# Second stage of blocks 2 and 3: where VectorE's sums for the next block, ScalarE's modulation pairs and one PSUM copy stand in their engines' orders

## Chip, core and metric

The kernel runs on one core of one Trainium2 chip. The metric is the device time of one execution in microseconds (us). Before the change it is 259.0 us (median of three runs, 258.9 to 259.67). All arithmetic is in fp32.

## What is computed

`x` holds 64 batches of 64 tokens with 512 features, 4096 token rows in all. Cut to what matters:

```python
q  = relu(cond @ W3 + b3)                          # 64 x 512
v  = (64 * x + x.sum(tokens)) * q[:, None, :]      # "modulation"
y  = relu(v @ W2 + b2)                             # first product, 512 x 512
g  = softmax(y @ W_router + b_router)              # 6 experts
w  = g kept for the two best experts, else 0
out = x + y @ W_base + b_base + (y @ A_s) @ B_s \
        + sum over experts e of w[e] * (y @ A_r[e]) @ B_r[e]
```

There are two large products, with W2 and with W_base. The rest is narrow: rank 16 for each of seven groups, six router columns.

## The kernel before, in words

Features lie on the 128 partitions, so the 512 features are four chunks; token rows lie along the free dimension. The rows are worked in four blocks (the loop over `k`, 0 to 3) of 1024 rows, two halves of 512. A block has a **first stage** (`first_inner`: modulated x times W2, then relu into `y`) and a **second stage** (the narrow product `ph`, the gate, and y times W_base plus the routed part).

Both large products use the seven-multiplication (Strassen-Winograd) form on 2x2 blocks, P1 to P7. In blocks 2 and 3 most of these P are themselves made by seven products of quarter blocks. In the code, `order` lists the outer products, `t` counts them, and `q(n, t)` is inner product n of the t-th one: two fp32 matmuls of 128x128 by 128x256 in the trace. Each outer product owns two PSUM banks, `ha`/`hb` in the second stage (`ia`/`ib` in the first). Its parts leave PSUM through small steps of `inner_tools`: `seed_y` (L987) and `seed_z` (L990) copy a half bank on ScalarE so that later products add to it; `take_w5`, `take_u`, `take_11`, `take_21` (all through `take`, L995) copy a quarter to SBUF on ScalarE; `take_12` and `take_22` (through `add`, L972) add a quarter on VectorE. TensorE may only overwrite or add to a quarter when the step that reads it is done.

The price of that form are sums of operands. For y they are made by GpSimd (`inner_sums`, L344 to L347) and VectorE (`row_sums`, L280 to L283). The sums for the **next** block's first stage, and the modulation of the next block's x, have no place of their own: they are put between the second stage's instructions. Two lists hold them.

* `behind` holds ScalarE's modulation, mostly in pairs (two activations, L229, each 128x64). `fill(n)` (L293) emits the next n entries.
* `held` holds VectorE's part: sums over tokens (`vsum`, L219 and L221), row sums `s` of feature chunk 0 (`early`, four instructions of 128x512, L280 to L283), the four inner sums `first` (128x256, L344 to L347), eight modulation steps of 128x64 (L227), three row sums of chunk 1, and four inner sums of 128x768 (L344 to L347). `sums_ahead(n)` (L298) emits the next n. One of the 28 entries allots two tiles and emits nothing.

The order is written by hand: each engine executes its instructions in the order in which the program emits them, and waits on semaphores for the others. There is no planner.

`second_between` (L712) is the second stage of blocks 2 and 3; its `main_part` (L785) is what the change edits. With `order = (1, 2, 4, 5, 3)`, t = 0 is P1, t = 1 is P2, t = 2 is P4, t = 3 is P5 and t = 4 is P3. P6 and P7 are plain products (`oy`, `oz`, L181) that are seeded with P1 by ScalarE (`seed`, L752). `with_x` adds x on VectorE and sends a row out on SyncE's queue. `to_rows` (L742) adds a finished P to the output rows in HBM by an accumulating DMA from GpSimd's queue; the second one adds to the rows of the first, so it waits until that has landed. `turn` transposes the weighted narrow product (`pt`, L647) and copies it to `hwT` (L649); `difference` (L654) is GpSimd's. Block 4 has no next block; it uses `second_inner`, which shares `inner_tools` only.

Of the kernel before, what the change touches and what calls it, by code (L numbers as in the profile page):

```python
# [38 lines left out]
def adaln_ffn(ctx: ExitStack, tc: tile.TileContext, xa, x0, x1, head, w3, w2, wb, a, bcat, bb, br, outT):  # L39
# [139 lines left out]
    def product(ps, i, j, w, s, start=True):  # L179
        for c in range(KH):  # L180
            nc.tensor.matmul(  # L181
                ps, w[i][:, c, ts(j, P)], s[i][:, c, :], start=start and c == 0, stop=c == KH - 1,
                skip_group_check=True,
            )
# [87 lines left out]
    def row_sums(a, name, cols=slice(0, TB)):  # L272

        all_s = mid.tile([P, 4, KH, TB], F32, tag=name, name=name)
        s = [all_s[:, i, :, cols] for i in range(4)]
        a11, a12, a21, a22 = a[:, :KH, 0, cols], a[:, KH:, 0, cols], a[:, :KH, 1, cols], a[:, KH:, 1, cols]

        def steps(c=slice(0, KH), fourth=nc.vector):
            return [
                lambda: nc.vector.tensor_tensor(s[0][:, c], a21[:, c], a22[:, c], ALU.add),  # L280
                lambda: nc.vector.tensor_tensor(s[1][:, c], s[0][:, c], a11[:, c], ALU.subtract),
                lambda: nc.vector.tensor_tensor(s[2][:, c], a11[:, c], a21[:, c], ALU.subtract),
                lambda: fourth.tensor_tensor(s[3][:, c], a12[:, c], s[1][:, c], ALU.subtract),  # L283
            ]

        return {1: a11, 2: a12, 3: s[3], 4: a22, 5: s[0], 6: s[1], 7: s[2], "sums": all_s}, steps
# [6 lines left out]
    def fill(n):  # L293
        for _ in range(min(n, len(behind))):
            for step in behind.pop(0):
                step()

    def sums_ahead(n):  # L298
        for _ in range(min(n, len(held))):
            held.pop(0)()  # L300
# [342 lines left out]
    def turn(k):  # L643
        pt = ps_h.tile([P, 2 * NS, P], F32, tag="ph", name=f"pt_{k}")
        hwT = small.tile([P, 2, TB], F32, tag="hwT", name=f"hwT_{k}")
        for s in range(2 * NS):
            nc.tensor.transpose(pt[:GB, s, :], hw[:, s, :], ident)  # L647
        for h in range(2):
            nc.scalar.copy(hwT[:GB, h], pt[:GB, ts(h, NS)].rearrange("p s t -> p (s t)"))  # L649
        return hwT  # L650

    def difference(k, hwT):
        hwd = small.tile([P, TB], F32, tag="hwd", name=f"hwd_{k}")
        nc.gpsimd.tensor_tensor(hwd[:GB], hwT[:GB, 0], hwT[:GB, 1], ALU.subtract)  # L654
        return hwd
# [56 lines left out]
    def second_between(k, y, res):  # L712


        order = (1, 2, 4, 5, 3)
        lo, hi = slice(0, R2), slice(R2, TB)
        of_y = {1: y[:, :KH, 0], 2: y[:, KH:, 0], 4: y[:, KH:, 1]}
        x12, x21, x22 = res[1, 0], res[0, 1], res[1, 1]
        plain = mid.tile([P, 4, 4, R2], F32, tag="inner_s", name=f"inner_y_{k}")
        sy, sy_steps = row_sums(y, "sy")  # L720
        sy_steps = sy_steps()

        of_sy = lambda n: sy["sums"][:, n].rearrange("p k t -> p (k t)").rearrange("p (n t) -> p n t", n=4)
        places = {o: plain[:, n] for n, o in enumerate((1, 2, 4))} | {5: of_sy(1), 3: of_sy(2)}
        s_side, sums_of = row_places(lambda o: of_y.get(o, sy[o]), {o: (t, (0, 1, 2, 3)) for o, t in places.items()})
        parts = {1: wide["parts"][:, 0], 2: wide["parts"][:, 1], 4: y[:, :KH, 1], 5: y[:, :KH, 0], 3: y[:, KH:, 0]}
        tools = inner_tools(k, "h", order, wide["t"], s_side, dict.fromkeys(order), parts)
        q, open_banks, bank, add = tools.q, tools.open_banks, tools.bank, tools.add
        hws = {}
        routed_of = {2: ("first", 0), 4: ("second", 0), 5: ("second", KH), 3: ("less", KH)}  # L730
        routed = with_routed(order, tools, hws, routed_of)

        def run(steps):
            for step in steps:
                step()

        def inner_sums(o):
            a = of_y.get(o, sy[o])
            run(sums_of(o, lambda c, r: a[:, c, ts(r, R2)], nc.gpsimd))

        def to_rows(o, f, h):
            nc.gpsimd.dma_start(  # L742
                outT[k, f : f + KH, h].rearrange("f p t -> p f t"), parts[o], accum_op=ALU.add
            )

        def with_x(x, name, j, f, h):
            add(x[:, j], bank[name, j], x[:, j])
            nc.sync.dma_start(outT[k, f + j, h], x[:, j])

        def seed(j, name, source):  # L750
            bank[name, j] = ps_p.tile([P, TB], F32, tag="pp", name=f"o{name}_{k}_{j}")
            nc.scalar.copy(bank[name, j], source)  # L752

        def start(t):
            open_banks(t)
            q(1, t)
            q(5, t)
            tools.seed_y(t)
            tools.take_w5(t)

        def sixth(t):
            q(6, t)
            tools.seed_z(t)
            tools.take_u(t)

        def seventh(t):
            q(7, t)
            routed(t, 22)
            tools.take_22(t)

        def second_and_third(t):
            q(3, t)
            q(2, t)

        def ends(t):
            routed(t, 1)
            tools.take_1(t)
            q(4, t)
            routed(t, 4)
            tools.take_21(t)  # L780

        for o in (1, 2):
            inner_sums(o)

        def main_part(ph):  # L785
            open_banks(1)
            q(1, 1)
            q(5, 1)
            tools.seed_y(1)

            def first():
                q(7, 0)
                q(3, 0)
                q(6, 1)
                tools.seed_z(1)
                q(2, 0)
                tools.take_11(0)
                tools.take_w5(1)
                tools.take_22(0)

            gate(k, ph, (first, lambda: tools.take_12(0)))
            q(4, 0)
            tools.take_21(0)
            second_and_third(1)
            weigh(k, ph)
            for j in range(KH):
                seed(j, "y", parts[1][:, j])
                product(bank["y", j], 6, j, tb, sy, start=False)
            fill(2)
            tools.take_u(1)  # L810
            sums_ahead(2)
            for j in range(KH):
                seed(j, "z", bank["y", j])
                with_x(x12, "y", j, KH, 0)

            for o in (5, 4):
                inner_sums(o)
            fill(2)
            product(bank["z", 0], 7, 0, tb, sy, start=False)
            with_x(x22, "z", 0, KH, 1)  # L820
            with_x(x21, "z", 0, 0, 1)
            hwT = turn(k)
            hws["first"], hws["second"] = (hwT[:GB, h] for h in range(2))
            product(bank["z", 1], 7, 1, tb, sy, start=False)
            with_x(x22, "z", 1, KH, 1)
            seventh(1)
            with_x(x21, "z", 1, 0, 1)
            hws["less"] = difference(k, hwT)[:GB]
            inner_sums(3)
            start(2)  # L830
            fill(2)
            ends(1)
            to_rows(1, 0, 0)
            to_rows(2, 0, 0)
            sums_ahead(4)
            sixth(2)
            fill(2)
            start(3)
            seventh(2)
            sums_ahead(5)  # L840
            second_and_third(2)
            sixth(3)
            fill(2)
            ends(2)
            to_rows(4, 0, 1)
            sums_ahead(8)
            start(4)
            seventh(3)
            sums_ahead(3)
            second_and_third(3)  # L850
            sixth(4)
            ends(3)
            to_rows(5, KH, 0)
            to_rows(5, KH, 1)
            sums_ahead(1)
            seventh(4)
            sums_ahead(3)
            second_and_third(4)
            ends(4)
            last_part.append(lambda: to_rows(3, KH, 0))  # L860

        return {
            "sums": lambda: run(sy_steps), 6: lambda: start(0), 7: lambda: sixth(0), "all": main_part
        }
# [515 lines left out]
```

## Time and profile before

| | |
|---|---|
| median of three runs | 259.0 us |
| the profiled execution, its own time | 258.9 us |
| its span from first to last instruction | 257.1 us |
| TensorE busy | 249.0 us (97%) |
| VectorE busy | 201.8 us (79%) |
| ScalarE busy | 156.5 us (61%) |
| GpSimd busy | 123.6 us (48%) |
| granted TensorE clock | 0.999 |
| block 2's stretch from its narrow product to the next first stage | 94.6 to 133.0 us |
| block 3's | 156.4 to 194.8 us |

PE is TensorE's matmul, PEld its weight load, DVE is VectorE, ACT ScalarE, POOL GpSimd, SP SyncE. A line of the timeline gives the start within the span, the duration, the engine, the source line, what is written from what, the shape, the number of instructions merged in the row, and in brackets the idle time just before and what ended it. Ends of matmuls are modelled, so two following rows of PE overlap by some 0.16 us. A row's duration on an engine also contains the time in which the instruction, once started, waits for something inside.

### The profile page before, as it was taken

What the parts mean: (1) busy time and instruction counts of PE and PEld (TensorE: products, weight loads), DVE (VectorE), ACT (ScalarE), POOL (GpSimd) and SP (SyncE); (2) the same over time, 40 slices, a digit from 0 to 9 for tenths busy, and PEclk for the clock granted to TensorE, in tenths of its full rate; (3) what the DMA queues carried; (4) which work ended last, traced back from release to release, by engine and by line L of the source; (5) the groups of instructions that cost most, each with busy time, mean ns of one, the idle gap of its engine ahead of it and who ended that gap; (6) DMA issues with size and microseconds to landing.
All of it is one profiled execution on the core that took longest, in us unless ns stands there. A gap on an engine that the chain in (4) does not pass through costs nothing.

```text
span 257.1 us, 3663 instructions
## 1 busy us (share of the span) xinstructions
PE 249.0 (97%) x1126; PEld 188.0 (73%) x1126; DVE 201.8 (79%) x405; ACT 156.5 (61%) x435; POOL 123.6 (48%) x150
## 2 busy tenths in 40 slices
PE   7999999999999999999998999999999999999994
PEld 3756896454467889657886888956788889975783
DVE  2899898699995887876897777996789576787472
ACT  2399496596049798767636889675855427442220
POOL 1000000029408686079269778219539995039850
PEclk9999999999999999999999999999999999999999
DMA  6998636003220044843598522305559553500054
GB/s 197 361 346 310 263 112 214 0 3 122 97 107 0 14 149 147 308 176 113 82 167 162 82 83 98 125 25 204 86 87 193 93 96 142 166 1 0 3 184 144
DMA packets 17339, 33.82 MB, mean 132 GB/s; under 512 B 1590, under 2 KB 3638, under 8 KB 17319
## 3 DMA queue, kind: packets, MB, share of 16 engines
q1 hardware_dynamic: 13766, 27.03, 29.6%
q0 software_dynamic: 3264, 6.29, 15.6%
q10 hardware_dynamic: 288, 0.26, 0.3%
q8 instruction: 9, 0.15, 0.2%
q14 instruction: 12, 0.09, 0.1%
HBM read 19.94 MB, written 14.68 MB: 135 GB/s over the span
## 4 chain that ended last, share of the span: by engine, by line
PE 74%; DVE 12%; ACT 10%; DMA 2%; issue 1%; SPq 0%; ACTq 0%
PE ph L1317 11%; PE ia L502 10%; PE ib L502 8%; PE ha L979 6%; PE py L409 5%; ACT x L229 5%; PE oy L181 5%; PE oz L181 5%; PE hb L979 5%; PE ja L979 4%; PE jb L979 4%; PE ox L181 3%; DVE inner_s L346 2%; DMA w_sb<-in_w_dram 2%; PE yw L181 1%; PE pt L647 1%
## 5 line engine op out<-in xcount | busy, mean ns | idle before, releaser
L229 ACT ACTIVATE x<-x,vsum,nq 128x64 f32<-128x64 f32 x176 | 62.9, 431 | 3.4 <-DVE vsum L221 3.4
L1317 PEld LDWEIGHTS ph<-a_sb,y 128*128 128x128 f32 x256 | 30.9, 192 | 1.6 <-ACT y L395 0.7
L1317 PE MATMUL ph<-a_sb,y 128*128 128x118 f32 x256 | 31.4, 276 | 0.3 <-ACT y L395 0.3
L654 POOL TENSOR_TENSOR hwd<-hwT 113x512 f32<-113x512 f32 x4 | 5.1, 1268 | 54.7 <-ACT hwT L649 54.7
L493 DVE TENSOR_TENSOR u<-ib,u 128x256 f32<-128x256 f32 x42 | 16.4, 418 | 7.9 <-PE ib L502 7.9
L493 DVE TENSOR_TENSOR u<-ia,u 128x256 f32<-128x256 f32 (+1 forms) x36 | 16.0, 462 | 7.7 <-ACT u L540 6.4
L502 PE MATMUL ib<-inner_s,inner_t 128*128 128x256 f32 x60 | 18.0, 388 | 0.2
L508 ACT COPY ib<-ia 128x256 f32<-128x256 f32 x21 | 7.6, 360 | 17.3 <-PE ia L502 17.3
L395 ACT ACTIVATE y<-u,head_sb 128x256 f32<-128x256 f32 (+1 forms) x30 | 15.8, 584 | 3.6 <-DVE u L468 3.0
L219 DVE TENSOR_REDUCE vsum<-x 128x8 f32<-128x512 f32 x24 | 15.4, 674 | 0.0
L181 PE MATMUL oz<-sy,tb 128*128 128x512 f32 x32 | 15.0, 592 | 0.0
L409 PE MATMUL py<-v,w_sb 128*128 128x512 f32 (+1 forms) x40 | 14.4, 510 | 0.6 <-DMA w_sb<-in_w_dram 0.6
L181 PE MATMUL oy<-sy,tb 128*128 128x512 f32 x32 | 14.6, 594 | 0.0
L502 PEld LDWEIGHTS ib<-inner_s,inner_t 128*128 128x128 f32 x60 | 11.0, 190 | 3.1 <-ACT ib L508 1.0
L511 ACT COPY ib<-ib 128x256 f32<-128x256 f32 x21 | 7.6, 364 | 8.5 <-PE ib L502 8.5
L344 POOL TENSOR_TENSOR sy<-sy 128x256 f32<-128x256 f32 x4 | 2.9, 727 | 20.5 <-PE oy L181 20.5
L742 POOL DMA_DIRECT2D out_dram<-y x8 | 10.7, 1450 | 3.5 <-issue 1.9
L267 ACT ACTIVATE v<-x,vsum,nq 128x64 f32<-128x64 f32 x32 | 11.1, 429 | 1.7 <-DVE vsum L265 1.7
L409 PEld LDWEIGHTS py<-v,w_sb 128*128 128x128 f32 x40 | 7.4, 190 | 6.3 <-issue 4.8
L972 DVE TENSOR_TENSOR xu<-oz,xu 128x512 f32<-128x512 f32 x12 | 7.9, 686 | 4.9 <-PE oz L181 4.8
L181 PEld LDWEIGHTS oy<-sy,tb 128*128 128x128 f32 x32 | 5.9, 190 | 6.6 <-issue 6.2
L502 PE MATMUL ia<-s,t 128*128 128x256 f32 x36 | 10.2, 379 | 0.0
(310 smaller groups left out, 669.8 us busy)
## 6 DMA issues: line engine op xcount, KB each, us to landing
xu<-in_x_dram SPq DMA_DIRECT2D x14, 512.0 KB, 4.4
out_dram<-xu SPq DMA_DIRECT2D x25, 256.0 KB, 2.1
x<-in_x_dram SPq DMA_DIRECT2D x12, 512.0 KB, 7.5
out_dram<-y POOLq DMA_DIRECT2D x8, 512.0 KB, 7.9
out_dram<-inner_tb POOLq DMA_DIRECT2D x4, 512.0 KB, 5.8
x<-in_x_dram SPq DMA_DIRECT2D x7, 256.0 KB, 5.6
w_sb<-in_w_dram SPq DMA_DIRECT2D x4, 256.0 KB, 6.0
wb_sb<-in_wb_dram SPq DMA_DIRECT2D x4, 256.0 KB, 5.0
```

What stands on the lines that cost most here:

```text
L181: nc.tensor.matmul(ps, w[i][:, c, ts(j, P)], s[i][:, c, :], start=start and c == 0, stop=c == KH - 1, skip_group_check=True,)
L219: nc.vector.tensor_reduce(vsum[:, c, bs], xc, AX.XY, ALU.add)
L229: nc.scalar.activation(x, x, AF.Identity, bias=bias, scale=scale)
L267: nc.scalar.activation(v[:, c, :, ts(b, NH)], batches_of(c, b, b + 1)[:, :, 0], AF.Identity, bias=vsum[:, c, b : b + 1], scale=nq[:, c, b ...
L395: nc.scalar.activation(y[:, f, h, cols], src, AF.Relu, bias=b2_sb[:, f : f + 1])
L409: nc.tensor.matmul(p[:, :, lo * NH : hi * NH], w2_sb[:, c, ts(f, P)], v[:, c, :, lo * NH : hi * NH], start=(c == 0 and lo == 0), stop=(c = ...
L493: add = lambda o, a, b: nc.vector.tensor_tensor(o, a, b, ALU.add)
L502: nc.tensor.matmul(bank[b, t][:, cols], t_side(o, n), s_side(o, n), start=n == 1, stop=True, skip_group_check=True,)
L742: nc.gpsimd.dma_start(outT[k, f : f + KH, h].rearrange("f p t -> p f t"), parts[o], accum_op=ALU.add)
L972: add = lambda o, a, b, engine=nc.vector: engine.tensor_tensor(o, a, b, ALU.add)
L979: nc.tensor.matmul(p, w, s, start=start, stop=True, skip_group_check=True)
L1317: nc.tensor.matmul(ph[:, h * NS + s, :HC], y[:, c, h, ts(s, P)], a_sb[:, c, :], start=(c == 0), stop=(c == NC - 1),)
```

## The change

Three things in `second_between`, so in blocks 2 and 3 alone. The same instructions are emitted, in another order.

* P2's `take_w5(1)` stands ahead of P1's `take_11(0)`.
* ScalarE's modulation: of the entries that stood after `start(2)` (2), `sixth(2)` (2) and `sixth(3)` (2), one goes between the two seeds of the y and z products, two go behind `turn`, and the other three stand singly after `sixth(2)`, `second_and_third(2)` and `sixth(3)`.
* VectorE's sums: in place of 4, 5, 8, 3, 1, 3 entries at six places there are now 1 and 2 between the x additions of the z product, 6 after the first two `to_rows`, 8, 3, 2, 1 and 1.

```diff
                 tools.seed_z(1)
                 q(2, 0)
+                tools.take_w5(1)
                 tools.take_11(0)
-                tools.take_w5(1)
                 tools.take_22(0)
...
                 seed(j, "z", bank["y", j])
                 with_x(x12, "y", j, KH, 0)
+                if j == 0:
+                    fill(1)
...
             with_x(x21, "z", 0, 0, 1)
+            sums_ahead(1)
             hwT = turn(k)
             hws["first"], hws["second"] = (hwT[:GB, h] for h in range(2))
+            fill(2)
             product(bank["z", 1], 7, 1, tb, sy, start=False)
             with_x(x22, "z", 1, KH, 1)
             seventh(1)
             with_x(x21, "z", 1, 0, 1)
+            sums_ahead(2)
             hws["less"] = difference(k, hwT)[:GB]
             inner_sums(3)
             start(2)
-            fill(2)
             ends(1)
             to_rows(1, 0, 0)
             to_rows(2, 0, 0)
-            sums_ahead(4)
+            sums_ahead(6)
             sixth(2)
-            fill(2)
+            fill(1)
             start(3)
             seventh(2)
-            sums_ahead(5)
+            sums_ahead(8)
             second_and_third(2)
+            fill(1)
             sixth(3)
-            fill(2)
+            fill(1)
             ends(2)
             to_rows(4, 0, 1)
-            sums_ahead(8)
+            sums_ahead(3)
             start(4)
             seventh(3)
-            sums_ahead(3)
+            sums_ahead(2)
             second_and_third(3)
             sixth(4)
             ends(3)
...
             sums_ahead(1)
             seventh(4)
-            sums_ahead(3)
+            sums_ahead(1)
             second_and_third(4)
             ends(4)
```

On each engine the order then differs as follows. TensorE, GpSimd and SyncE keep their orders, DMA issues included. VectorE keeps the order among the sums and among the PSUM additions and mixes the two otherwise: L280 stands between the x additions of `oz`'s first half and those of its second, L281 and L282 before P2's `take_12`, L283 and the four of `first` before P4's `take_22`, the eight L227 between P4's two additions, the three row sums of chunk 1 before P5's `take_22`, two of the 128x768 sums before P5's `take_12`, one before and one after P3's `take_22`. ScalarE runs two L229 between the `oz` seeds and four right after the `hwT` copies, none between P4's `take_w5` and P2's `take_11`.

## Prediction

> **What bounds the kernel now.** I read the page's first and fourth parts, then TensorE's waits and its timeline, because the chain runs 74% through TensorE.
>
> ```profile
> span 257.1 us, 3663 instructions
> PE 249.0 (97%) x1126; PEld 188.0 (73%) x1126; DVE 201.8 (79%) x405; ACT 156.5 (61%) x435; POOL 123.6 (48%) x150
> PE 74%; DVE 12%; ACT 10%; DMA 2%; issue 1%; SPq 0%; ACTq 0%
> ```
>
> TensorE is nearly always busy, so an edit that leaves its instructions alone is worth only the gaps it closes. In the timeline of block 2's second stage and the start of the next block they are these, with one matmul (123.92) that has no gap yet:
>
> ```profile
> 106.88 0.67 PE L979 MATMUL ha<-inner_y,wb_sb 128*128 128x256 f32 x2 [0.40 <-ACT inner_tb L995]
> 120.81 0.67 PE L979 MATMUL hb<-inner_y,inner_tb 128*128 128x256 f32 x2 [0.33 <-ACT y L995]
> 123.92 0.60 PE L979 MATMUL hb<-y,inner_tb 128*128 128x256 f32 x2
> 139.65 0.70 PE L502 MATMUL ib<-x,inner_t 128*128 128x256 f32 x2 [1.01 <-DVE u L493]
> 141.28 0.70 PE L502 MATMUL ib<-inner_s,inner_t 128*128 128x256 f32 x2
> ```
>
> Rows follow each other at 0.43 per pair when nothing waits. Row ib at 139.65 follows one at 138.04, so it is 139.65 - 138.47 = 1.18 late; the one at 141.28 follows 140.61, so 0.24 late. A check: the stretch 133.0 to 155.6 (block 3's first stage up to its narrow product) takes 22.6, the same work in block 4, 194.8 to 216.0, takes 21.2; 22.6 - 21.2 = 1.4 = 1.18 + 0.24. Block 4 has no next block to prepare. Block 3's second stage repeats block 2's two small gaps (168.67 and 182.61), with no large one after it.
>
> Why the large gap? VectorE's timeline, then GpSimd's:
>
> ```profile
> 119.75 0.42 DVE L972 TENSOR_TENSOR inner_tb<-ha,inner_tb 128x256 f32<-128x256 f32 x1 [2.10 <-ACT inner_tb L995]
> 120.09 0.94 DVE L280 TENSOR_TENSOR s<-x 128x512 f32<-128x512 f32 x1
> 122.88 0.41 DVE L972 TENSOR_TENSOR y<-hb,y 128x256 f32<-128x256 f32 x1
> 132.68 3.12 DVE L346 TENSOR_TENSOR inner_s<-s 128x768 f32<-128x768 f32 x1
> 135.72 1.48 DVE L347 TENSOR_TENSOR inner_s<-s,inner_s 128x768 f32<-128x768 f32 x1
> 139.17 0.42 DVE L493 TENSOR_TENSOR u<-ib,u 128x256 f32<-128x256 f32 x1
> ```
> ```profile
> 119.75 0.73 POOL L347 TENSOR_TENSOR sy<-sy 128x256 f32<-128x256 f32 x1
> 132.72 2.25 POOL L283 TENSOR_TENSOR s<-x,s 128x512 f32<-128x512 f32 x1
> 135.05 1.33 POOL L344 TENSOR_TENSOR inner_s<-s 128x256 f32<-128x256 f32 x1
> ```
>
> L346 takes 3.12 where its two sisters take 0.95: it sits behind GpSimd's L283 for 2.25. Then GpSimd's L344 needs 1.33 instead of 0.73, and L347 1.48: the two engines take turns. So VectorE reaches the addition L493, which frees the bank for TensorE, at 139.17 instead of about 137.2. Two sums with both inputs in SBUF collide with GpSimd; additions with one input in PSUM don't.
>
> **The parts.** *(1) `take_w5(1)` ahead of `take_11(0)`.* TensorE's row at 106.88 waits for the second of two copies that start at 106.09 and, by ScalarE's spacing, 106.36. First in line, `take_w5(1)` waits for nothing and starts at 105.93, after `seed_z(1)` (105.66 + 0.27), ends by 106.3, and TensorE goes on at about 106.45. But 0.87 later it needs `oy`, seeded by ScalarE (0.58) after `take_11(0)` and `take_21(0)`. These still wait for TensorE; the seed moves from 107.04 to 106.94 at best. TensorE starts `oy` at 106.94 + 0.58 + 0.14 (the latency from copy to matmul seen at 106.88) = 107.66 instead of 107.82. Most of the 0.4 reappears there: gain 0.15 (0.05 to 0.16). `take_12(0)` and the gate behind it move 0.3 later; `hw` is then ready at 110.2, TensorE's transposes come at 112.97. Free.
>
> *(2) ScalarE's pairs.* The four L229 before `take_11(1)` (1.3 us) made `seed_z(2)` start at 119.88 although its product was done at 119.62. Without them it starts 0.04 behind it (as at 123.21/123.25), 119.66; `take_u(2)` ends 0.22 earlier and the row at 120.81 moves to 120.6: gain 0.2 (0.15 to 0.25). Their new places are idle: 1.15 before the second `oz` seed (two need 0.75) and 2.38 behind the `hwT` copies (four need 1.35). At zero cost as long as these waits stay; the remaining pairs stand singly where 0.7 is idle.
>
> *(3) VectorE's sums, end of the stage.* Three 128x768 sums leave the place just before P3's last addition; one stays. Chaining the row durations from P4's `take_22` (below, 123.65): eight L227 1.8, `take_12(2)` 0.34, three row sums 1.9, `take_22(3)` 0.35, L344 and L345 1.8, `take_12(3)` 0.35, L346 0.86, `take_22(4)` 0.4, L347 0.86: 132.3. GpSimd's L283 comes after its DMAs, see (5), at 132.6. So L346 is no longer caught. Then `take_12(4)` to 132.9, nq 0.3, token sums 1.2, their scaling at worst behind L283 at 134.9. L493 has its product only at 137.2, so over 2 us are spare; even L347 caught for 2.25 would leave TensorE unhindered. Both late rows vanish: gain 1.42, once, in the stage behind block 2 (behind block 3 nothing waits).
>
> *(4) VectorE's sums, middle.* Here is the price. L280, L281, L282, L283 and `first` move from 120.09-124.7, when GpSimd has nearly finished its sums, into 114.4-123, beside GpSimd's unbroken row (110.64 to 120.42). Eight sums now stand ahead of P4's `take_22`, four before; and TensorE's row at 123.92 waits for it. The nearest rows are block 1's, where such sums already collide:
>
> ```profile
> 63.08 1.10 DVE L281 TENSOR_TENSOR s<-s,x 128x512 f32<-128x512 f32 x1
> 64.10 1.21 DVE L282 TENSOR_TENSOR s<-x 128x512 f32<-128x512 f32 x1
> 63.70 1.05 POOL L152 TENSOR_TENSOR inner_tb<-tb,inner_tb 128x256 f32<-128x256 f32 x1
> 64.72 1.18 POOL L153 TENSOR_TENSOR inner_tb<-tb 128x256 f32<-128x256 f32 x1
> ```
>
> One VectorE sum of 128x512 plus one GpSimd sum take 1.13 together (64.10 to 65.23), 0.60 of it VectorE's own; GpSimd's share is 0.55. In turns: L280 at 114.9 to 115.5, inside VectorE's 1.30 of idle time. GpSimd slips by 0.45, its `difference` holds until 117.93. L281 to 118.53, GpSimd 119.08, L282 119.68, (`take_12(1)` beside GpSimd) 120.23, L283 120.83, GpSimd 121.38, L344 121.72, GpSimd's last 122.27, L345 to L347 at 0.34 each 123.29, `take_22(2)` 0.41: 123.70, TensorE 0.06 later at 123.76. It wants that row at 123.92 - 0.2 = 123.72 (part 1 moves both). Stall 0.04, with eight turns of some 0.03 uncertainty each in my reading: I book 0.1.
>
> The Trainium skill, page "SBUF — State Buffer", section "Who interferes with whom", says that a VectorE instruction with two SBUF inputs and a GpSimd instruction that reads SBUF exclude each other and that whoever came first holds the port for its whole instruction. The trace agrees on the exclusion; on the length, "whole" would be the 0.73 of GpSimd's row instead of 0.55. With four such turns, `take_22(2)` ends near 124.4 and the stall is 0.74 in each block. I take 0.55, since it is measured under collision; the rule's 0.74 stays as the upper end, and no collision at all (stall 0) as the lower.
>
> *(5) GpSimd's queue.* Nothing in it is moved, but its sums end 1.9 later (122.3), so `to_rows(1)` issues then; the second waits for its landing (120.42 to 126.84 before: 6.4), hence 128.7; then 129.4, and the P5 pair at 131.1, just after its data (130.75). L283 and the sums for products 3 and 2 follow 1.5 later, at 132.6 (132.72 before). TensorE needs product 2's first sum at 145.27 and GpSimd had it at 139.84, so some 4 us of cover remain after TensorE's gain. Free. SyncE's row writes stay behind their additions, which don't move.
>
> **The sum.** Per block -0.15 - 0.2 + 0.1 = -0.25, twice -0.5; once -1.42: -1.9. The profiled execution took 258.9 (257.1 of span, 1.8 around it), so 257.0; the median is 0.1 above it: **257.1**.
>
> **Rivals.** *(A) The port is held as the rule says:* stall 0.74, per block +0.39, in all -1.42 + 0.78 = -0.6: 258.4. For it: L283 held it for all of 2.25. Against: the four rows above.
> *(B) GpSimd always wins:* VectorE's sums from L281 on wait for the end of its row at 120.9; then 0.6 + 0.6 + 0.34 + 0.6 + 1.36 + 0.41 end at 124.8, TensorE 1.15 late, per block +0.8: -1.42 + 1.6, so 259.2, slower than before. It turns the sign when `take_22(2)` ends after 124.6; below that the large gap pays. Against it: GpSimd's L344 at 135.05 had to let L346 go first.
> *(C) The large gap stays in part:* L347 and the scaling of the token sums are both caught, and L493 comes at 138 or later; gain 0.4 of 1.42: 258.1 to 258.5. Against it: 2 us spare.
>
> **Chances and range.** Main 0.66, A 0.15, B 0.08, C 0.11. The main case alone runs from 256.7 (no stall, upper gains) to 257.8. The range 256.5 to 258.6 takes in A and C and leaves out B and some tail. A change of 0.3% (0.8 us) is about what this measurement can tell from none. Faster by more: main and a little of A and C, 0.69; within: most of A and C, half of B, 0.22; slower: half of B and what I haven't thought of, 0.09.
>
> **What would show it.** (1) The 0.40 gap before `ha` shrinks and a gap of some 0.2 appears before `oy`. (2) The 0.33 gap falls to about 0.1. (3) L346 takes 0.95, and no gap follows `ib<-x` in the next block; that first stage takes 21.2. (4) VectorE's L281 to L283 show about 1.1 each, GpSimd's four `sy` sums beside them above 1; a gap before `hb<-y` of 0 to 0.2. A gap of 0.7 there means A. (5) The first accumulating DMA is issued about 2 us later. The prediction is wrong if a longer gap appears before `hb<-y`, or if L493 is again what the next block waits for.

## The result

| | before | after |
|---|---|---|
| median of six runs, us | 258.95 (258.47 to 259.67) | 257.0 (256.87 to 257.28) |
| profiled execution, us | 258.9 | 257.28 |
| its span, us | 257.1 | 255.5 |

The ratio of after to before is 0.9924, with a 95% interval of 0.9909 to 0.9939. The forecast was 257.1.

From the pages, the shares of the chain that ended last in before, and then the head, the busy times and the same shares of after:

```profile
PE 74%; DVE 12%; ACT 10%; DMA 2%; issue 1%; SPq 0%; ACTq 0%
```
```profile
span 255.5 us, 3660 instructions
PE 249.9 (98%) x1126; PEld 188.2 (74%) x1126; DVE 202.0 (79%) x405; ACT 157.4 (62%) x435; POOL 125.2 (49%) x150
PE 86%; DVE 7%; ACT 5%; issue 1%
```

The work on every engine is nearly what it was; GpSimd is busy 1.6 us longer (125.2 against 123.6). The chain has changed: TensorE's share of it went from 74% to 86%, so fewer of its links are waits for the other engines.

To see where the time went, I cut the trace at rows that every version has. A "second stage" runs from the first matmul of the narrow product `ph` to the first `ia` (in before from 93.83; the 94.6 of the table ahead is where `ph` goes on behind a wait of its own), the "first stage" of the next block from there to its `ph`. In after, everything up to block 2's second stage is 0.54 us later than in the profile of before (`ph` starts at 94.37 against 93.83). That lies ahead of anything that was changed, so stages are compared and not clock times.

| us | block 2, second | block 3, first | block 3, second | block 4, first |
|---|---|---|---|---|
| before | 39.18 | 22.62 | 39.17 | 21.01 |
| after | 38.92 | 21.00 | 38.93 | 21.00 |
| difference | -0.26 | -1.62 | -0.24 | -0.01 |

Together that is -2.13 us by the stages, against -1.95 between the medians. The engines' busy time in the first two of these stretches, for before and then for after (stretch, its length, then the busy time of each engine with its count of instructions, the granted clock, the DMA share and GB/s):

```profile
93.83:133.01 39.18, 38.29 (x193) 30.69 (x192) 31.23 (x63) 26.88 (x75) 21.51 (x27) 1.00 0.59 165
133.01:155.63 22.62, 21.54 (x98) 17.91 (x97) 18.30 (x39) 17.69 (x53) 18.04 (x20) 1.00 0.58 110
```
```profile
94.37:133.29 38.92, 38.66 (x194) 30.58 (x193) 35.19 (x65) 27.29 (x75) 23.06 (x27) 1.00 0.54 155
133.29:154.29 21.00, 21.00 (x97) 18.07 (x96) 14.69 (x37) 17.74 (x53) 17.22 (x20) 1.00 0.75 139
```

In after, TensorE (the first busy number) fills all of the first stage. VectorE (the third) is busy 4 us longer in the second stage and 3.6 us less in the first. That is partly work that moved, and partly sums that take longer beside GpSimd. The clock is full in both, so no throttle is in this.

TensorE's timeline of after, the rows that answer to those shown of before:

```profile
106.98 0.67 PE L984 MATMUL ha<-inner_y,wb_sb 128*128 128x256 f32 x2
108.10 3.70 PE L181 MATMUL oy<-sy,tb 128*128 128x512 f32 x8
120.95 0.67 PE L984 MATMUL hb<-inner_y,inner_tb 128*128 128x256 f32 x2
124.09 0.70 PE L984 MATMUL hb<-y,inner_tb 128*128 128x256 f32 x2
138.75 0.59 PE L502 MATMUL ib<-x,inner_t 128*128 128x256 f32 x2
```

None of them has a bracketed wait any more. Smaller ones are left, which show only in the distance between starts (0.43 where nothing waits). The row at 120.95 follows one at 120.28, so it is 0.24 late. The one at 124.09 is 0.03 late. The last, `ib<-x`, follows 138.32 at 0.43: the large wait of 1.01 is gone. VectorE's and then GpSimd's timeline of after:

```profile
117.95 1.08 DVE L281 TENSOR_TENSOR s<-s,x 128x512 f32<-128x512 f32 x1
118.95 1.21 DVE L282 TENSOR_TENSOR s<-x 128x512 f32<-128x512 f32 x1
123.63 0.41 DVE L977 TENSOR_TENSOR y<-hb,y 128x256 f32<-128x256 f32 x1
130.53 0.95 DVE L346 TENSOR_TENSOR inner_s<-s 128x768 f32<-128x768 f32 x1
137.66 0.42 DVE L493 TENSOR_TENSOR u<-ib,u 128x256 f32<-128x256 f32 x1 [1.98 <-PE ib L502]
```
```profile
118.44 1.17 POOL L344 TENSOR_TENSOR sy<-sy 128x256 f32<-128x256 f32 x1
119.69 1.06 POOL L345 TENSOR_TENSOR sy<-sy 128x256 f32<-128x256 f32 x1
122.70 1.33 POOL L742 DMA_DIRECT2D out_dram<-inner_tb  x1
132.64 2.99 POOL L283 TENSOR_TENSOR s<-x,s 128x512 f32<-128x512 f32 x1
```

VectorE's L281 and L282 take 1.08 and 1.21, where they took 0.69 and 0.68 in before, and GpSimd's sums 1.06 to 1.17 instead of 0.73: that is the price of the new place. L346 takes 0.95 instead of 3.12, since VectorE is through with it before GpSimd's L283 starts. And L493, which had been what TensorE waited for, now waits 1.98 us for TensorE.

GpSimd's L283 itself did not become shorter: 2.99 in after, with none of VectorE's large sums beside it, and 2.25 in before. It stands right behind accumulating DMA issues, here of before and then of after:

```profile
131.23 2.44 POOL L742 DMA_DIRECT2D out_dram<-y  x2 [1.95 <-issue]
```
```profile
130.15 4.18 POOL L742 DMA_DIRECT2D out_dram<-y  x3
```

In both blocks of before, of after and of every version below, L283 ends 1.30 us behind the end of these rows, to the hundredth or two (133.67 to 134.97 in before, 134.33 to 135.63 in after). So a good part of its length (0.95 in before, 1.69 in after) is time behind the DMA issues. The issues alone did not hold VectorE's sums up: L346 of after takes 0.95 beside them. In before L346 was held to the end of L283 (134.97, and its own 0.83 more). Why it was not served in the 0.95 us in which L283 still stood behind the issues isn't shown.

### The profile page after: what moved, and what is told of

It is laid out like the page before. It is cut to its first block, busy times and chain, and to the rows that moved or that the text cites. A ratio compares the mean times of both kernels' runs of the same rounds, so it can differ in the third digit from the quotient of the medians.

```text
span 255.5 us, 3660 instructions
## 1 busy us (share of the span) xinstructions
PE 249.9 (98%) x1126; PEld 188.2 (74%) x1126; DVE 202.0 (79%) x405; ACT 157.4 (62%) x435; POOL 125.2 (49%) x150
## 4 chain that ended last, share of the span: by engine, by line
PE 86%; DVE 7%; ACT 5%; issue 1%
PE ia L502 11%; PE ph L1322 11%; PE ha L984 10%; PE ib L502 9%; PE hb L984 8%; PE oy L181 6%; PE py L409 6%; PE oz L181 5%; PE ja L984 4%; PE jb L984 4%; ACT x L229 3%; PE ox L181 3%; PE idle L192 1%; PE yw L181 1%; PE pt L647 1%; PE yx L416 1%
## 5 line engine op out<-in xcount | busy, mean ns | idle before, releaser
L229 ACT ACTIVATE x<-x,vsum,nq 128x64 f32<-128x64 f32 x176 | 63.3, 431 | 1.6 <-DVE vsum L221 1.6
L493 DVE TENSOR_TENSOR u<-ib,u 128x256 f32<-128x256 f32 x42 | 16.5, 420 | 14.1 <-PE ib L502 14.1
L493 DVE TENSOR_TENSOR u<-ia,u 128x256 f32<-128x256 f32 (+1 forms) x36 | 16.0, 464 | 7.7 <-ACT u L540 6.3
L344 POOL TENSOR_TENSOR sy<-sy 128x256 f32<-128x256 f32 x4 | 3.8, 950 | 20.2 <-PE oy L181 20.2
L742 POOL DMA_DIRECT2D out_dram<-inner_tb x4 | 4.9, 1234 | 10.6 <-DVE inner_s L344 5.4
```

The lines of the kernel that those rows point to most:

```text
L229: nc.scalar.activation(x, x, AF.Identity, bias=bias, scale=scale)
L493: add = lambda o, a, b: nc.vector.tensor_tensor(o, a, b, ALU.add)
L742: nc.gpsimd.dma_start(outT[k, f : f + KH, h].rearrange("f p t -> p f t"), parts[o], accum_op=ALU.add)
```

## The experiments

The theory is that of the prediction: the second stage is TensorE's own work plus the waits at `oy`, `hb<-inner_y` and `hb<-y`; the first stage of the next block is TensorE's work plus what VectorE's late row makes it wait; two engines that both add from SBUF take turns. Line numbers shift by a few from kernel to kernel (the addition of L972 is L975, L977 or L981 in others). Each run was timed beside the kernel before, and a ratio is to that.

| | time, us | ratio, interval | block 2, second | block 3, first | block 3, second |
|---|---|---|---|---|---|
| swap alone | 258.79 | 0.9988 (0.9979 to 0.9996) | 39.03 | 22.41 | 39.02 |
| pairs alone | 258.1 | 0.9952 (0.9939 to 0.9964) | 38.92 | 21.80 | 38.93 |
| sums alone | 257.52 | 0.9931 (0.9917 to 0.9945) | 39.18 | 21.00 | 39.17 |
| sums, only the end | 258.82 | 0.9988 (0.998 to 0.9997) | 39.79 | 21.00 | 39.79 |
| swap and pairs | 257.42 | 0.9927 (0.99 to 0.9954) | 38.78 | 21.80 | 38.78 |
| after + four additions | 259.12 | 0.9997 (0.9979 to 1.0015) | 39.77 | 22.19 | 39.19 |
| after + nine fills | 259.51 | 1.0003 (0.9985 to 1.0021) | 38.92 | 23.41 | 38.33 |
| after + two additions | 258.74 | 0.9996 (0.9978 to 1.0015) | 39.76 | 21.00 | 39.74 |
| after + four fills | 256.96 | 0.9925 (0.9912 to 0.9939) | 38.93 | 21.00 | 38.93 |
| waits closed, U late | 257.26 | 0.9914 (0.9882 to 0.9946) | 38.96 | 21.01 | 38.96 |
| waits filled | 256.07 | 0.9896 (0.9879 to 0.9913) | 38.53 | 21.00 | 38.55 |

**One part at a time.** First the swap of the two copies, made in the kernel before:

```
                 q(2, 0)
+                tools.take_w5(1)
                 tools.take_11(0)
-                tools.take_w5(1)
                 tools.take_22(0)
```

> Only P2's take_w5 ahead of P1's take_11; sums and pairs as before. Theory (three separate gains, one price): the wait before ha shrinks by 0.3 and a wait of about 0.2 opens before oy, so 0.15 to 0.26 per block, 0.3 to 0.5 in all: 258.4 to 258.7. Rival (the seed of oy takes the whole gain back): 258.9, and oy starts no earlier relative to the narrow product.

Each second stage is 0.15 us shorter, as reckoned, although `oy` starts 0.25 earlier (13.74 after `ph` instead of 13.99). ScalarE writes `oy`'s seed in two halves, and the seeds moved by only 0.11; what came earlier at the start of the eight matmuls is lost in part inside them (3.70 instead of 3.60). The first stage behind block 2 is 0.21 shorter as well: VectorE's eight L227 take 1.87 instead of 2.27 (in before the last of them, beside a DMA issue of GpSimd, took 0.72 against 0.31 for most), and L493 comes 0.20 earlier against the end of the stage. How much of this is the swap's doing isn't shown.

Then ScalarE's pairs alone:

```
                 with_x(x12, "y", j, KH, 0)
+                if j == 0:
+                    fill(1)
...
+            fill(2)
             product(bank["z", 1], 7, 1, tb, sy, start=False)
...
             start(2)
-            fill(2)
             ends(1)
...
             sixth(2)
-            fill(2)
+            fill(1)
             start(3)
...
             second_and_third(2)
+            fill(1)
             sixth(3)
-            fill(2)
+            fill(1)
             ends(2)
```

> Only ScalarE's modulation pairs as in the changed kernel; sums and the copy of P2's W as before. Theory: the row hb<-inner_y (120.81 before) comes 0.2 earlier in each block, nothing else moves: 258.5. Rival (the pairs are what closes the large gap, because the token sums' scaling and the first L229 of the next block come earlier): the gap of 1.2 before ib<-x goes too, 257.2.

This is a miss. The second stages gain 0.26, near the 0.2 reckoned, but the next block's first stage also falls by 0.82 us, where I had expected nothing. One more row of VectorE's timeline of before, and then TensorE's and VectorE's timelines of this run:

```profile
125.69 0.42 DVE L972 TENSOR_TENSOR y<-ha,y 128x256 f32<-128x256 f32 x1 [0.93 <-ACT y L995]
```
```profile
139.16 0.70 PE L502 MATMUL ib<-x,inner_t 128*128 128x256 f32 x2 [0.20 <-DVE u L493]
```
```profile
119.34 0.43 DVE L975 TENSOR_TENSOR inner_tb<-ha,inner_tb 128x256 f32<-128x256 f32 x1 [1.11 <-ACT inner_tb L998]
119.68 1.25 DVE L280 TENSOR_TENSOR s<-x 128x512 f32<-128x512 f32 x1
120.97 1.10 DVE L281 TENSOR_TENSOR s<-s,x 128x512 f32<-128x512 f32 x1
125.35 0.42 DVE L975 TENSOR_TENSOR y<-ha,y 128x256 f32<-128x256 f32 x1 [0.28 <-ACT y L998]
132.14 3.17 DVE L346 TENSOR_TENSOR inner_s<-s 128x768 f32<-128x768 f32 x1
138.68 0.42 DVE L493 TENSOR_TENSOR u<-ib,u 128x256 f32<-128x256 f32 x1
```

The large wait went from 1.01 to 0.20 although L346 is held as long as before (3.17). Two of VectorE's additions say why. This profile starts 0.58 later, by `ph`, which is taken off here. `take_12(1)` waits for `take_11(1)` on ScalarE, and in the kernel before that copy stood behind four L229; now VectorE waits 1.11 us instead of 2.10 and starts the addition at 118.76 instead of 119.75. Most of that is lost again: L280 and L281 now stand beside GpSimd's last sums and take 1.25 and 1.10 instead of 0.94 and 0.69, and `take_22(2)` starts only 0.26 earlier. `take_12(2)`, the row at 125.69, waits for P4's `take_11(2)` in the same way. That copy stood behind four L229 as well and now stands behind two; the wait falls from 0.93 to 0.28, and the addition starts at 124.77, 0.92 earlier. From there on VectorE's row stays about 1 us ahead (L493 at 138.10 against 139.17). So ScalarE's pairs held up not just one TensorE row but also VectorE, and through it the next block. That is read from the rows; the two places of the pairs were not moved one by one.

Then VectorE's sums alone, swap and pairs as before:

```
             with_x(x21, "z", 0, 0, 1)
+            sums_ahead(1)
             hwT = turn(k)
...
             with_x(x21, "z", 1, 0, 1)
+            sums_ahead(2)
             hws["less"] = difference(k, hwT)[:GB]
...
-            sums_ahead(4)
+            sums_ahead(6)
             sixth(2)
...
             seventh(2)
-            sums_ahead(5)
+            sums_ahead(8)
             second_and_third(2)
...
-            sums_ahead(8)
+            sums_ahead(3)
             start(4)
             seventh(3)
-            sums_ahead(3)
+            sums_ahead(2)
             second_and_third(3)
...
             seventh(4)
-            sums_ahead(3)
+            sums_ahead(1)
             second_and_third(4)
```

> Only VectorE's sums as in the changed kernel; pairs and the copy as before. Theory: the late rows of the next block's first stage vanish (1.42, once), and P4's take_22 is in time for hb<-y since TensorE comes there 0.35 later than in the changed kernel: 257.5. If the two engines held the port for GpSimd's whole 0.73, a wait of 0.4 would stand before hb<-y in each block: 258.3.

As expected, and 0.2 us more: the whole 1.62 us of the first stage, and no cost in the second stage. TensorE's timeline:

```profile
121.27 0.67 PE L981 MATMUL hb<-inner_y,inner_tb 128*128 128x256 f32 x2 [0.33 <-ACT y L997]
124.37 0.60 PE L981 MATMUL hb<-y,inner_tb 128*128 128x256 f32 x2
```

The old wait at `hb<-inner_y` still stands, and it hides the late sums: `hb<-y` comes without one.

Could the end be spread without the early start beside GpSimd? From the kernel before, with the old start and the new end:

```
             seventh(2)
-            sums_ahead(5)
+            sums_ahead(13)
             second_and_third(2)
...
-            sums_ahead(8)
+            sums_ahead(3)
             start(4)
             seventh(3)
-            sums_ahead(3)
+            sums_ahead(2)
...
             seventh(4)
-            sums_ahead(3)
+            sums_ahead(1)
```

> VectorE's sums stay as before up to P4's take_22 (no early start beside GpSimd), and only what follows is spread: after it nine entries with the eight L227, then three row sums, then the 128x768 sums two, one, one. Pairs and the copy as before. Theory: the large gap closes (-1.42), but VectorE is now late in the middle: first to 124.7, L227 to 126.5, take_12(2) to 126.8, three row sums to 128.7, P5's take_22 to 129.1, while TensorE needs it at 128.68: a wait of 0.5 before the second hb<-sy of P5 in each block, 258.5. Rival (the early start beside GpSimd is needless, the spread at the end does it all): 257.5 and no such wait.

The first stage is again 21.00, but each second stage is 0.61 us longer. TensorE's timeline shows a bracketed wait that no other version has:

```profile
129.34 0.70 PE L979 MATMUL hb<-sy,inner_tb 128*128 128x256 f32 x2 [0.35 <-DVE y L972]
```

VectorE cannot do all of it behind P4 without holding up P5's addition. The early sums buy the room at the end.

**Do the gains add?** The change with VectorE's sums put back where they were, that is, swap and pairs together:

> The changed kernel with VectorE's sums put back to their old places: only the copy and the pairs moved. Theory: second stages as short as their two gains allow, 0.15 + 0.26 each without the price of the collision; in the next block's first stage the large gap is back, but only in part (about 0.7 of 1.6), because the earlier take_11(1) lets VectorE's whole row start 1.0 earlier: 257.6. Rival (the gap is closed by the sums alone): 258.2 and a gap of 1.6 less 0.2.

Second stages of 38.78: -0.15 and -0.26 add up to within 0.01. The first stage is 21.80, as with the pairs alone; of the two additions named there, the expectation knew only the first. The difference between this version and after is what the sums' move is worth once the rest is there: 38.92 - 38.78 = +0.14 and 38.93 - 38.78 = +0.15 in the second stages, -0.80 in the first stage, together -0.51 by the stages. Alone it was worth 1.62. The pairs and the sums cure the same wait, so their gains overlap.

**What the neighbour on GpSimd costs.** To test the turns, four GpSimd additions on a spare tile were put into after, behind its sums of P4, so that VectorE's last sums ahead of `take_22(2)` meet them as well:

```
             inner_sums(3)
+            for _ in range(4):
+                nc.gpsimd.tensor_tensor(spare, spare, spare, ALU.add)
             start(2)
```

> The changed kernel with four more GpSimd additions of 128x256 (both inputs in SBUF, into a spare tile that nothing else reads) behind its last four sums, so that VectorE's last first sums meet them too. Theory (they take turns at about 0.55 for GpSimd's share): L346 and L347 are each held up once, P4's take_22 ends 1.1 later than in the changed kernel, and since TensorE already waits 0.14 for it, the stage grows by 1.1 in blocks 2 and 3: 259.2. Rival (GpSimd holds the port for its whole 0.73): 1.5 per block, 260.0. Rival (no exclusion; the rows of about 1.1 have another cause): 257.0.

As a control, nine fills of the same tile at the same place, which keep GpSimd busy about as long and read nothing:

```
             inner_sums(3)
+            for _ in range(9):
+                nc.gpsimd.memset(spare, 0.0)
             start(2)
```

> The same with nine GpSimd memsets of 128x256 in that place instead (they write and read nothing), some 2.5 us of GpSimd work. Theory (the exclusion is of reads): VectorE's sums run as in the changed kernel, only the accumulating DMAs leave later: 257.0. Rival (GpSimd being busy, or the later DMAs, is what costs): 259 or more, like the run with four additions.

The additions gave nearly the time that turns had promised (259.12 against 259.2), but not for that reason alone: block 2's second stage grew by 0.85 us and not by 1.1, and the first stage got 1.19 us longer. The control missed by 2.5 us. Its second stage of block 2 is to the hundredth that of after, so the fills did not disturb VectorE. The time is in the first stage, in the timelines of GpSimd, VectorE and TensorE:

```profile
121.73 3.38 POOL L838 MEMSET spare<- 128x256 f32 x9
149.19 2.49 POOL L600 TENSOR_TENSOR inner_late<-u,u 128x512 f32<-128x512 f32 x2
```
```profile
150.49 0.42 DVE L493 TENSOR_TENSOR inner_late<-ia,inner_late 128x256 f32<-128x256 f32 x1 [2.24 <-POOL inner_late L600]
154.30 0.43 DVE L493 TENSOR_TENSOR u<-ia,u 128x256 f32<-128x256 f32 x1 [1.79 <-POOL u L603]
```
```profile
154.78 0.70 PE L502 MATMUL ia<-inner_late,t 128*128 128x256 f32 x2 [1.09 <-DVE u L493]
```

Everything behind the fills in GpSimd's queue came later, and its products L600 and L603 in the next block became what VectorE waits for. They started at 149.19 - 93.41 = 55.78 after `ph`, in after at 146.03 - 94.37 = 51.66: 4.12 later. TensorE lost 2.41 of it, so about 1.7 us had been spare. (Block 4's first stage lost another 0.82.) Of the 2.41, TensorE won back 0.59 in block 3's narrow product, which is this, first in after and then with nine fills:

```profile
154.29 0.60 PE L1322 MATMUL ph<-a_sb,y 128*128 128x118 f32 x4
155.05 1.77 PE L1322 MATMUL ph<-a_sb,y 128*128 128x118 f32 x12 [0.16 <-ACT y L395]
```
```profile
155.74 1.95 PE L1326 MATMUL ph<-a_sb,y 128*128 128x118 f32 x16
```

In after the product waits inside for ScalarE's `y`; the one that starts late doesn't. That alone makes block 3's second stage, as it is cut here, shorter in these two versions: 38.33 is 38.92 less 0.59, and 39.19 is 39.77 less 0.58. Both runs thus mixed two effects. The next pair keeps the lateness under that spare time, and equal: two additions against four fills.

> The partner of the run with four fills: two additions on a spare tile (0.77 us each, from the four that took 3.07 us) at the same place, so that GpSimd's queue is late by the same 1.5 us. Theory (two operations that both read the on-chip memory take turns): VectorE's L346 and L347 of the first half take 0.83 us instead of 0.41, hb<-y goes 0.8 us later, second stages 39.7 (as with four additions, since only these two sums meet them), first stage 21.0: 257.0 + 2 x 0.8 = 258.6 us. Rival (only the lateness counts): like the run with the fills.

> Made from the changed kernel: four fills of a spare tile (0.375 us each, from the nine that took 3.38 us) in GpSimd's queue behind its sums of P4, in each of the two blocks. They delay what is queued behind them by 1.5 us, like two additions would, but read nothing. Theory (fills leave VectorE's sums alone; GpSimd's queue has spare time before its products L600 hold anyone up: with the nine fills those products came 4.1 us later and TensorE's first stage lost 2.41 us, so some 1.7 us are spare): second stages 38.92, first stage 21.0, time as that of the changed kernel, 257.0 us. Rival (every us of GpSimd's lateness costs its share, 2.41 / 3.38 = 0.71): 1.1 us more in the first stage, 258.1 us. Rival (a fill holds VectorE up as an addition does): second stages over 39.5.

Both came out as the theory had it, 1.78 us apart with the same first stage. With two additions, VectorE's, GpSimd's and TensorE's timelines:

```profile
123.21 0.83 DVE L346 TENSOR_TENSOR inner_s<-x 128x256 f32<-128x256 f32 x1
123.96 0.83 DVE L347 TENSOR_TENSOR inner_s<-x,inner_s 128x256 f32<-128x256 f32 x1
```
```profile
122.96 1.54 POOL L838 TENSOR_TENSOR spare<-spare 128x256 f32<-128x256 f32 x2
```
```profile
125.17 0.70 PE L988 MATMUL hb<-y,inner_tb 128*128 128x256 f32 x2 [0.71 <-DVE y L981]
```

With four fills, VectorE's and GpSimd's:

```profile
122.58 0.41 DVE L346 TENSOR_TENSOR inner_s<-x 128x256 f32<-128x256 f32 x1
122.92 0.41 DVE L347 TENSOR_TENSOR inner_s<-x,inner_s 128x256 f32<-128x256 f32 x1
```
```profile
122.32 1.41 POOL L838 MEMSET spare<- 128x256 f32 x4
```

The same two VectorE sums at the same place take 0.83 beside an addition and 0.41 beside a fill, and TensorE's `hb<-y` waits 0.71 or not at all. So it is GpSimd's additions that hold VectorE up, not GpSimd being busy. Beside additions the two sums start 0.75 apart instead of 0.34: the neighbour's share is 0.41.

**A version that closes what is left.** Two tries at the waits that after still has. The first, made from after:

```
             tools.take_21(0)
+            q(7, 1)
             second_and_third(1)
...
-            seventh(1)
+            routed(1, 22)
+            tools.take_22(1)
...
-            sums_ahead(6)
-            sixth(2)
+            sums_ahead(4)
+            q(6, 2)
+            tools.seed_z(2)
             fill(1)
             start(3)
-            seventh(2)
-            sums_ahead(8)
+            q(7, 2)
+            tools.take_u(2)
+            routed(2, 22)
+            tools.take_22(2)
+            sums_ahead(10)
             second_and_third(2)
```

> The changed kernel with its three remaining gaps of the second stage taken on: P2's seventh product issued ahead of its third (covers the waits before ha and oy, 0.3), P4's take_u emitted behind its seventh product (so that this no longer waits for that copy, 0.24), and two of first moved behind P4's take_22 (no wait before hb<-y, 0.14). Theory: 0.69 per block, 1.4 in all: 255.6. Rival (the waits move on to the next row that needs the same engines): 256.6 to 257.0.

This was a miss in size: the stage stayed at 38.96. TensorE's and ScalarE's timelines:

```profile
121.41 0.70 PE L990 MATMUL hb<-hwT,bcat_sb 113*128 113x256 f32 x2 [0.67 <-ACT y L1006]
```
```profile
120.42 0.37 ACT L998 COPY hb<-ha 128x256 f32<-128x256 f32 x1
120.99 0.37 ACT L1006 COPY y<-hb 128x256 f32<-128x256 f32 x1
```

P4's U (`y<-hb`) is now copied behind a pair and two other copies instead of right behind the seed, and the next product of that bank waits for it. The 0.24 us before `hb<-inner_y` had not been closed but moved one product on, and had grown. The rest worked: `oy` starts 13.78 after `ph` with one product more ahead of it (0.43), against 13.73, so 0.38 us of small waits were filled. The second try keeps that and puts another ready product into the wait instead. (The products that its edit moves are P2's seventh, `q(7, 1)`, and P4's third, `q(3, 2)`; the expectation names P5 and P2.)

```
             tools.take_21(0)
+            q(7, 1)
             second_and_third(1)
...
-            seventh(1)
+            routed(1, 22)
+            tools.take_22(1)
...
-            sums_ahead(6)
+            sums_ahead(4)
             sixth(2)
             fill(1)
             start(3)
+            q(3, 2)
             seventh(2)
-            sums_ahead(8)
-            second_and_third(2)
+            sums_ahead(10)
+            q(2, 2)
```

> The three waits that the changed kernel still has in its second stage, each filled: P5's seventh product ahead of its third and second (the small waits before oy: 0.38 us, from the earlier run that did this among other things), P2's third product ahead of its seventh (the wait of 0.24 us before hb<-inner_y), and two of VectorE's sums behind P4's last addition (the 0.10 us before hb<-y). Theory (the second stage is TensorE's own work and these waits, nothing else): 38.92 - 0.38 - 0.24 - 0.10 = 38.20 us per second stage, first stage 21.0, time 257.0 - 1.45 = 255.6 us. Rival (a wait that is filled comes back behind the next operand, as when P2's U left late and 0.67 us stood before hb<-hwT): 256.5 to 257.0 us with a bracketed wait in the same stage.

At 256.07 us it is the best version here. Its second stages are 0.39 and 0.38 us shorter than those of after, of the 0.72 expected; TensorE's timeline has no bracketed wait behind `ph` in them, but these rows:

```profile
120.31 0.59 PE L987 MATMUL hb<-inner_y,inner_tb 128*128 128x256 f32 x2
123.02 0.70 PE L987 MATMUL hb<-y,inner_tb 128*128 128x256 f32 x2
128.07 0.70 PE L987 MATMUL hb<-sy,inner_tb 128*128 128x256 f32 x2
```

`hb<-inner_y` follows its forerunner at 0.44: that wait is gone. But `hb<-y` is 0.11 late (0.03 in after), since TensorE comes for it sooner, and `hb<-sy` at 128.07 is 0.19 late, which it was not in after. About half of the gain came back as waits further on.

## Why the prediction was right

*(1) The swap.* Booked -0.15 per block, measured -0.15 alone, and -0.14 in the company of the pairs (38.78 against 38.92). The place was right too: the wait before `ha` shrank to 0.13, and another of 0.18 stands before `oy` (107.49 to 108.10 is 0.61).

*(2) The pairs.* Booked -0.2 per block, measured -0.26. The step "their new places are idle, at zero cost" held. What it lacked was what else waited for copies behind L229: VectorE's `take_12(1)`, and above all `take_12(2)`. The line that I showed of the first carried the wait, 2.10 behind ScalarE's `inner_tb`, and I passed over it; the second, with its 0.93, I hadn't looked at. The pairs alone are worth 0.82 us once in the first stage.

*(3) The end of the stage.* Booked -1.42, measured -1.62. L346 at 0.95, L493 with 2 us to spare and no wait behind `ib<-x` are as forecast. The size was off by 0.2 since I added two late rows and left out what follows each: after a row that waited, the next one starts 0.53 and not 0.43 later (139.65 to 140.18, 141.28 to 141.81), so 1.18 + 0.24 + 0.10 + 0.10 = 1.62. My check by block 4 had read its end at 216.0; the narrow product there starts at 215.81, which gives 22.62 - 21.01 = 1.61.

*(4) The middle.* Booked +0.1, measured +0.14: the row `hb<-y` is 0.03 late where I had worked out 0.04, and the row after it another 0.10. In my chain `take_22(2)` ended at 123.70 and TensorE wanted it at 123.72; it ended at 123.63 + 0.41 - 0.54 = 123.50, and TensorE would have come at 124.05 - 0.54 = 123.51. Both are 0.2 earlier, so the difference held; 0.15 of it is part 1's, which I had left out on both sides. The row that I took for the turn, 1.13 for one VectorE sum of 128x512 and one GpSimd sum, came again as 1.14 (118.95 to 120.09). Of the rule in the Trainium skill, page "SBUF — State Buffer", sections "Who interferes with whom" and "SBUF: two separate sides", one half is now shown here by a run of its own: GpSimd's additions exclude VectorE's sums and its fills, which only write, don't. The other half, that whoever came first holds on for its whole instruction, agrees with the rows of after, although the prediction read it otherwise. GpSimd's L344 ends at 118.44 + 1.17 = 119.61 and VectorE's L282 beside it at 118.95 + 1.21 = 120.16, so L282 was held to that end and then took 0.55; the rows of block 1 in the prediction have the same (64.75 and 65.31). What failed is the figure that I made of it, 0.73 for a turn, which had put the end of `take_22(2)` near 124.4. A GpSimd sum that had to wait takes less behind VectorE's than its step of 0.69 alone: L345 ends at 120.75, 0.59 behind L282. Why isn't shown.

*(5) GpSimd's queue.* The first accumulating DMA came at 122.70 - 0.54 = 122.16 (forecast 122.3), L283 at 132.10 (forecast 132.6). Free, as said; but I put the cover at some 4 us and it is less. The run with four fills shows that 1.41 us more cost nothing, the one with nine that 3.38 us more cost 2.41 in the first stage, of which 0.59 came back. I had looked at product 2's first sum; what comes due first is L600.

*The sum and the rivals.* -0.25, -0.25 and -1.42 against -0.26, -0.24 and -1.62. The large errors, (2) and (3), concern the same wait, so they did not add: it can vanish only once, and it did. That the total came within 0.1 us of the forecast is therefore in part luck: the 0.82 us that I had missed in (2) lay inside the wait that (3) closed anyway. Rival A (0.73 for each turn) and B (GpSimd always first) fall with `take_22(2)`, C with L493. Only the shares were wrong: by the same steps the pairs alone would have been worth 0.4 us, and they were worth 1.0 (259.13 for the kernel before beside them, 258.1).

Three things stay open: why a row after a waiting one starts 0.10 us late, what held L346 while GpSimd's L283 still stood behind the DMA issues, and why the part ahead of block 2's `ph`, which no version changes, ends anywhere from 93.41 (nine fills) to 94.81 (four additions) in the profiles.

## What to carry over

When instructions leave the front of copies on a shared engine, list everything that waits for each of these copies: here a TensorE row in the same stage, and two VectorE additions whose lateness decided the next one. Gains that end in one wait overlap, so try the parts alone before giving each its share: 0.82 and 1.62 us together made 1.62. In the two tries here a small wait was filled better by a ready product than by moving the late operand, which moved the wait; and even then about half came back at the next operands.

## What the runs showed of the hardware

GpSimd filling a tile does not slow VectorE's two-input sums at all (0.41 beside it, 0.41 alone), whereas GpSimd's additions double them (0.83). VectorE's sum is held to the end of GpSimd's row: in after L282 ends 0.55 behind the end of GpSimd's L344, and L281 and L283 as much behind the rows beside them. Where they collide, the pair takes less than the sum of both: 0.75 for two sums of 128x256 (0.34 + 0.69 = 1.03 alone), 1.14 for a VectorE sum of 128x512 with a GpSimd sum of 128x256 (0.60 + 0.69 = 1.29 alone).

A GpSimd addition of 128x512 that stood right behind accumulating DMA issues showed as a row of 2.25 to 3.27 us and ended 1.30 us behind the end of the issues in all 13 profiles. The neighbour's cost is therefore not 1.30: in before VectorE's L346 took 2.25 longer than its own 0.87.

A matmul row that follows one that waited starts 0.51 to 0.54 us after it instead of 0.43, in every place looked at. A wait therefore costs about 0.1 us more than the distance that shows before it.
